# A four-layer f32 network on one core: the feed-forward part of layer 2 multiplied by quarters of the tokens, its anchors by another order of operands, and the last weights turned in layer 0

## The chip, the cores and the metric

The kernel runs on one core of a Trainium2 chip. A core has these engines: TensorE (PE; its weight loads are shown apart as PEld), VectorE (DVE), ScalarE (ACT), GpSimd (POOL) and SyncE (SP), of which SP and POOL issue the transfers of this kernel. The metric is device time in microseconds (us), the median of three runs. All arithmetic is in f32.

## The reference

The input x is 8 blocks of 128 tokens with 512 channels (8, 128, 512). Four layers follow, and each adds its result to x. A layer is a conditioning part and then a feed-forward part:

```
x = x + L0_ffn(L0_cond(x))   # gated FFN of width 1376 with a lora per block; then base_W + 8 lora experts, top 2
x = x + L1_ffn(L1_cond(x))   # an adapter chosen per block; then 8 heads weighed by a softmax
x = x + L2_ffn(L2_cond(x))   # attention, 32 heads, cached and new keys; then see below
x = x + L3_ffn(L3_cond(x))   # W + gated experts; then 64 experts of rank 8, top 16
```

The change is about layer 2's feed-forward part and about weights of layer 3. Layer 2's part takes y2, attention's result projected by Wo, and computes

```
H = y2 @ W.T + b                          # (1024 tokens, 512)
z = y2 @ A                                # rank 32
anchors = every second token              # the odd ones
H_slice = H[anchors, :8];  delta_slice = z[anchors] @ LiMEs.T
logits = 0.5 * H_slice / max|H_slice| + 0.5 * delta_slice / max|delta_slice|
probs = softmax(logits);  weights = probs * sigmoid((probs - second largest) / 0.5), normalized
p_mix = (weights repeated for both tokens of a pair) @ LiMEs
out = H + ((z * p_mix) @ Bmat) * 0.5
```

The two maxima are taken over all anchors, so no weight is known before every block's y2 is.

## The kernel before, in words

x lies in SBUF with channels on the partitions (4 chunks of 128) and the 1024 tokens along the free axis. A product with a 512x512 matrix is 4 output chunks by 4 input chunks of f32 matmuls for each group of tokens. One f32 matmul stands in the trace as two records.

**Layer 0** is `forward` from L48 on. Its big products are done by seven products of sums of sub-blocks in place of eight: the class `Down` (L601 to L636) has the steps `begin`, `go_on` and `out`, and the matmuls are issued at L367 (`dn`, `g`, `gu`, `td`). Its weights live in the pool `w0`, with tiles tagged "Ad" and "Bg" among others; SP loads them. L655 to L684 are the end of layer 0, where VectorE prepares sums for `Down` and then has idle stretches. After layer 0, attention's first operands q and l are loaded, VectorE forms sums of them (`q_s`), and PE's first use is `q_one` (L985).

**Attention** (L807, its loop `run` L1332) has 32 steps: 8 groups of heads by 4 pairs of token blocks. A step projects the next step's q, k and v (`project` L1019, by seven products in `seven` L971: `q_one` to `q_six`), turns them through DRAM (`turned_new` written, then read as `qT` and `kn` by `fetch` L1163; the cached keys through `turned_cached` as `kT`, L1120), computes scores `st` (`weigh` L1171), and mixes values into `av` (`mix` L1226). The softmax sums are formed by VectorE, written to DRAM (`sums`), and read back on all partitions as their reciprocals `R` (`inverted` L1212). `divided` (L1237) multiplies `av` by `R` into `oT`, `outputs` (L1243) adds sums of `oT` (`os`), and `leave` (L1251) projects these by Wo into y2, again by seven products (`wo_one` to `wo_six`, L985). The order of instructions on every queue is that of the program text wherever `kept` is put around an instruction. Attention has three PSUM tags: "mm" and "st" with 3 banks, "av" with 2.

**Work of layer 2 inside attention's last steps.** `ending` (L1747) holds all of layer 2's feed-forward part and layer 3. From step 5 on `run` advances `prepare` (L1790) at two places of a step: it turns the 512x32 matrix A by four PE transposes (`A2Tp`), copies it to `A2T`, multiplies with LiMEs (`alp`, 4 matmuls), and thus has WH = [W's first 8 columns, A·LiMEs], 16 columns that give both slices of an anchor at once. In the last group of heads each step turns two finished blocks of y2 (`turn` L1813, four PE transposes a block into `y2T`). The step before the last then does the first half of z and of the anchors:

```
if n + 2 == len(steps):
    end.low(0, bank)
    end.anchors(0, bank)
```

After the loop stand the last `divided`, `outputs`, `product(0, "st")` (block 0's H), and `leave(31)`.

**`low`** (L1821) computes z for four blocks at once: A's 32 columns are the weights, and each block goes to a slot of 32 partitions, N = 128 tokens. **`anchors`** (L1830) takes y2T as weights (128 tokens that are every second column) and streams WH's 16 columns; the result `hd` has tokens on partitions, as routing wants it. **`product(b)`** (L1847): 16 matmuls with N = 128 into one bank of `[P, 4, 128]`.

**`layer2`** (L2201) turns the last two blocks, does the second half of z and anchors, then products of blocks 1 to 3, with `weights_turned` (L1977) advanced between: layer 3's 512x512 `base3` and the 512x128 `wB3` are loaded during attention's end by `open3` (L1947) and turned by PE (`W3p`, 16 transposes in 4 banks, and `wB3p`, 4), each bank copied by ACT. Then `routing` (L1861: `big` maxima on VectorE, `top` over the partitions on POOL, softmax with ACT, top 2, sigmoid, `p`), `gains` (L1910: p turned by PE to `pT`, `pmix` = pT by LiMEs, `zp` = z·pmix/2), the product of block 4, `delta(0)` (L1934: Bmat's 32 rows by zp added into the banks of blocks 0 to 3, which VectorE then adds to x), blocks 5 to 7 with `fold_scores` (L1991: `qwp`, `qbp`, `fkp`, `gkp`, which need the turned weights), and `delta(1)`. Banks: block 0 to 2 take "st", 3 and 4 take "av", the rest "mm".

**`layer3`** (L2233) begins with the sums of W3 on POOL (`weights_summed`) and the router matmuls `midp` (`midp_l`, 32 records with 128x200 operands), then products by seven (`last_begun`, `last`), each with VectorE adding to x and SP storing to `out`. After `scores(1)`, `sums_checked` (L762) tests whether every softmax sum lay in a safe interval; its last instruction is VectorE's cast of the flag to an integer, `redo_i`. SP reads that flag, and only if it is set would attention be repeated by a slower path, which does not happen here.

## Time and profile before

| What | Value |
|---|---|
| Median of three runs | 1488.01 us (1486.08, 1488.01, 1489.38) |
| The profiled execution's own time | 1486.79 us |
| Its span, first to last instruction | 1485.0 us |
| Granted clock of PE, mean | 0.999 |
| VectorE busy | 1063.70 us (72%) |
| ScalarE busy | 563.59 us (38%) |
| GpSimd busy | 856.36 us (58%) |
| Bytes moved by DMA | 172.29 MB, mean 116 GB/s |

PE's busy time by stretches of the span:

| Stretch, us | What runs | PE busy, us | DVE busy, us |
|---|---|---|---|
| 0 to 300 | layers 0 and 1, attention's beginning | 297.96 | 152.06 |
| 300 to 1306 | attention's steps | 1004.05 | 810.55 |
| 1306 to 1336 | the end of the step before the last, the last step | 29.14 | 15.63 |
| 1336 to 1386 | the last projection and layer 2's feed-forward part | 49.09 | 20.31 |
| 1386 to 1485 | layer 3 | 91.08 | 65.16 |

How to read the rows that follow. In the list of groups a row has the line, the engine, the operation, the output and input by their names in the program, PE's tiles (128*32 is 128 rows by 32 columns of weights; 128x128 after it the streamed operand, partitions by elements), the count, and then the busy time and the mean duration of one in ns, and the engine's idle time ahead of them. In the timeline a row has its start and its length in us, engine, line, operation and count, and in brackets the idle time before it and what ended that. Matmuls overlap: a row's length is longer than the distance to the next row's start. "Start to start" below is that distance divided by the number of records.

### The profile page before, as it was taken

Reading aid. Unit: us, or ns where it says so; the run is one execution under the profiler, and the core shown is the slowest. Engines: PE = TensorE matmul, PEld = TensorE weight load, DVE = VectorE, ACT = ScalarE, POOL = GpSimd, SP = SyncE. Lnnn points to the kernel's source line nnn. Section 1 sums busy time; section 2 is a strip of 40 time slices with the busy share of each in tenths; the row PEclk is TensorE's granted clock in tenths of the full one; section 3 lists DMA queues with packets and bytes.
Section 4 is the critical chain, followed back from the end, with each engine's and each line's share of the span. In section 5 each row is a group of like instructions: output and inputs, shape, how many; then the busy total and the mean of one; then the engine's idle time right before and its main releaser. Section 6 shows DMA issues by size and latency. Waiting matters only on the chain.

```text
span 1485.0 us, 18055 instructions
## 1 busy us (share of the span) xinstructions
PE 1471.3 (99%) x5571; PEld 934.6 (63%) x5571; DVE 1063.7 (72%) x2121; ACT 563.6 (38%) x1426; POOL 856.4 (58%) x876
## 2 busy tenths in 40 slices
PE   9999999999999999999999999999999999999998
PEld 7888786455556555555655555555555555558886
DVE  4665425478878787787888778787878878855475
ACT  1111110044445544444554454554445455431110
POOL 2241105477767777776777777777777777622310
PEclk9999999999999999999999999999999999999999
DMA  7411001214555544453454455345445534433001
GB/s 242 121 44 32 23 1 62 88 41 126 183 158 148 153 131 128 150 181 117 135 157 129 128 167 172 107 135 164 129 124 165 170 107 137 120 107 98 1 8 52
DMA packets 155993, 172.29 MB, mean 116 GB/s; under 512 B 52784, under 2 KB 126256, under 8 KB 155760
## 3 DMA queue, kind: packets, MB, share of 16 engines
q1 hardware_dynamic: 137712, 134.04, 30.6%
q0 software_dynamic: 17056, 36.49, 7.8%
q8 instruction: 47, 0.77, 0.2%
q10 hardware_dynamic: 1120, 0.52, 0.1%
q14 instruction: 58, 0.48, 0.1%
HBM read 129.95 MB, written 40.76 MB: 115 GB/s over the span
## 4 chain that ended last, share of the span: by engine, by line
PE 94%; DVE 3%; DMA 1%; issue 1%; ACT 0%; SPq 0%; DVEq 0%; ACTq 0%
PE st L1179 18%; PE av L1231 17%; PE g L367 9%; PE q_six L985 8%; PE q_one L985 6%; PE q_five L985 6%; PE wo_two L985 5%; PE dn L367 5%; PE wo_one L985 4%; PE wo_six L985 3%; PE eo_l L53 3%; PE h L1767 2%; PE z L1767 2%; PE o L1767 1%; PE midp_l L53 1%; PE gu L367 1%
## 5 line engine op out<-in xcount | busy, mean ns | idle before, releaser
L928 POOL DMA_INDIRECT kn<-in_k_cache,kvrow_k x256 | 272.1, 1063 | 77.2 <-issue 70.3
L928 POOL DMA_INDIRECT vals<-in_v_cache,kvrow_v x256 | 271.4, 1060 | 73.6 <-issue 59.6
L1231 PE MATMUL av<-pT,vals 128*128 128x512 f32 x640 | 290.8, 592 | 0.2 <-DVE oT L1241 0.2
L1183 ACT ACTIVATE pT<-st,hide 128x512 f32<-128x512 f32 x256 | 175.9, 687 | 191.9 <-PE st L1179 164.3
L1179 PE MATMUL st<-qT,kT 128*128 128x512 f32 x512 | 236.2, 594 | 0.3
L1231 PEld LDWEIGHTS av<-pT,vals 128*128 128x128 f32 x640 | 121.4, 190 | 152.7 <-issue 149.5
L1084 POOL TENSOR_TENSOR vq<-q,txq 128x256 f32<-128x256 f32 x128 | 121.1, 976 | 132.9 <-ACT sqq L1058 93.4
L1179 PEld LDWEIGHTS st<-qT,kT 128*128 128x128 f32 x512 | 96.3, 190 | 110.2 <-issue 105.0
L1199 DVE TENSOR_TENSOR part<-pT 128x512 f32<-128x512 f32 x128 | 88.3, 691 | 77.6 <-ACT pT L1183 64.5
L985 PE MATMUL q_one<-q,x 128*128 128x384 f32 x256 | 93.0, 486 | 0.0
L1058 ACT ACTIVATE sqq<-q 128x128 f32<-128x128 f32 x252 | 78.2, 310 | 10.6 <-DVE q L1034 4.0
L985 PEld LDWEIGHTS q_one<-q,x 128*128 128x128 f32 x256 | 48.5, 190 | 39.8 <-issue 14.1
L985 PE MATMUL q_six<-q_s,xs_all 128*128 128x384 f32 x192 | 69.8, 486 | 0.0
L1039 ACT COPY q<-q_one 128x256 f32<-128x256 f32 x32 | 11.9, 372 | 151.8 <-PE q_one L985 133.5
L985 PE MATMUL wo_one<-o,oT 128*128 128x256 f32 x256 | 65.8, 379 | 0.7 <-DVE oT L1241 0.7
L1179 PE MATMUL st<-qT,kTn 128*128 128x512 f32 x128 | 65.4, 592 | 0.0
L985 PE MATMUL wo_two<-o_s,os 128*128 128x256 f32 x256 | 60.6, 380 | 0.3 <-DVE os L944 0.3
L1183 ACT ACTIVATE pT<-st,rs 128x512 f32<-128x512 f32 x64 | 44.0, 687 | 38.6 <-PE av L1231 13.4
L985 PEld LDWEIGHTS wo_one<-o,oT 128*128 128x128 f32 x256 | 48.6, 190 | 14.2 <-DVE oT L1241 0.8
L436 POOL TENSOR_TENSOR ws<-wu 128x256 f32<-128x256 f32 (+1 forms) x9 | 6.4, 712 | 86.5 <-DMA wu<-in_WuT 86.5
L1215 ACT COPY rows<-rows 32x32 f32<-32x32 f32 x96 | 20.7, 216 | 93.0 <-DVE rows L1210 89.7
L367 PE MATMUL g<-xs,ws 128*128 128x256 f32 (+1 forms) x240 | 55.1, 379 | 0.0
(466 smaller groups left out, 2832.5 us busy)
## 6 DMA issues: line engine op xcount, KB each, us to landing
turned_new<-qkt SPq DMA_DIRECT2D x120, 160.0 KB
turned_cached<-kt SPq DMA_DIRECT2D x128, 128.0 KB
kT<-turned_cached SPq DMA_DIRECT2D x32, 512.0 KB
R<-sums SPq DMA_DIRECT2D x32, 512.0 KB
qT<-turned_new SPq DMA_DIRECT2D x30, 512.0 KB
q<-in_WqT SPq DMA_DIRECT2D x8, 1024.0 KB
o<-in_WoT SPq DMA_DIRECT2D x8, 1024.0 KB
kn<-in_k_cache,kvrow_k POOLq DMA_INDIRECT x256
```

The source lines that it names most:

```text
L53: pe.matmul(o, lhsT, rhs, start=start, stop=stop)
L367: pe.matmul(o, lhsT, rhs, start=start, stop=stop, skip_group_check=True)
L928: kept(pool.indirect_dma_start(out=d[:, c, :], out_offset=None, in_=kc if what == "k" else vc, in_offset=bass.IndirectOffsetOnAxis(ap=kvro ...
L985: kept(pe.matmul(o, l[:, c, :], r[:, c, :], start=start and c == 0, stop=c == 1, skip_group_check=True))
L1058: kept(act.activation(sq, S[n][m][:, j, i, :], AF.Square, accum_out=S[n]["ssq"][:, j, col : col + 1]))
L1084: kept(pool.tensor_tensor(to, t[:, b, :, hi : hi + 64], wx[:, b, lo : lo + 64].unsqueeze(2).to_broadcast(list(to.shape)), ALU.mult,))
L1179: kept(pe.matmul(ps, s["kT"][:, c, 4 * j : 4 * j + 4, :] if c < 4 else s["kn"][:, j], s["qT"][:, :, REP * j : REP * (j + 1), :].rearrange( ...
L1183: kept(act.activation(pT[:, c, :, :].rearrange("p i t -> p (i t)"), ps, AF.Exp, **(dict(bias=hide[:, b, c : c + 1]) if c < 4 else dict(bia ...
L1199: kept(dve.tensor_tensor(o, l, r, ALU.add))
L1215: kept(act.copy(rows[0:32, g, :], rows[32 * g : 32 * g + 32, 0, :]))
L1231: kept(pe.matmul(ps, v[:, c, :], pT[:, c, :, :].rearrange("p i t -> p (i t)"), start=c == 0, stop=c == NC - 1, skip_group_check=True,))
L1767: return pe.matmul(o, lhsT, rhs, start=start, stop=stop, skip_group_check=True)
```

## The change

- **Product by quarters.** `product(q)` takes a quarter of the tokens (N = 256) and half of the output chunks to a bank `[P, 2, 256]`: two banks a quarter, 8 matmuls (16 records) each, 16 matmuls a quarter. Quarter 0 is done ahead of the last `leave`, where block 0 was; quarters 1 and 2 follow in `layer2`. Quarter 3's banks receive `delta` first and the product after it. The additions to x are apart (`added(q)`, two a quarter).
- **Anchors weights first.** WH is widened with zeros to 32 columns and becomes the weights; the tokens of a quarter (every second column of y2T, 128 of 256) are streamed, four quarters in the four slots of 32 partitions: `hdT`, 16 matmuls. VectorE copies it, PE turns it back in one transpose (`hd`), and VectorE adds the bias. `low` is done once for all tokens between the two (N = 256, four quarters in four slots), and ACT copies z. Nothing of z or the anchors is left in the step before the last.
- **`delta`, `pmix`** work on quarters too: N = 256 and 128, Bmat's 32 rows of each slot.
- **Last weights turned by VectorE in layer 0.** `base3`, `wB3` and A are loaded in layer 0 into the free tiles "Ad" and "Bg", turned in squares of 32x32 by VectorE's transpose (six instructions), and stored by SP to three tensors in DRAM in such an order that the whole is turned (24 stores, one for each 32 partitions). Three places of layer 0 advance this. `open3` loads W3 and wB3T from there, and `prepare` loads A2T from there, with `alp` a step later. The 24 PE transposes and ACT's six copies of them go.
- **The order in `layer2`**: anchors with z between, products of quarters 1 and (first half) 2 with routing beside them, pT, `qwp` and `qbp`, `pmix`, the rest of quarter 2, `delta`, three additions, quarter 3 with `fkp` and `gkp` between its halves.
- **The check's cast** to `redo_i` is issued behind the last gate operation of `scores(1)`.

The diff, without the lines that only pass arguments on; of longer removed stretches, which stand in the kernel above, only the first line is shown:

```diff
@@ -65,6 +65,20 @@
     x = xpool.tile([P, DC, NT], F32, tag="x", name="x")
+    w3T, wB3T, A2T = (
+        nc.dram_tensor(n, shape, F32, kind="Internal").ap()
+        for n, shape in (("w3_turned", (D, D)), ("wB3_turned", (D, P)), ("A2_turned", (32, D)))
+    )
+    late_weights = [
+        (a["base3"][d * P : (d + 1) * P, :], w3T[:, d * P : (d + 1) * P].rearrange("(b i) (q j) -> q i b j", i=32, j=32))
+        for d in range(DC)
+    ]
+    late_weights.append((a["wB3"], wB3T.rearrange("(b i) (q j) -> q i b j", i=32, j=32)))
+    late_weights.append((
+        a["A2"].rearrange("(c p) r -> p c r", p=P), A2T.rearrange("i (c q j) -> q i c j", q=4, j=32)
+    ))
+    late_turned = w3T, wB3T, A2T
@@ -577,6 +591,22 @@
+        def weights_turned():
+            for n in range(0, len(late_weights), 2):
+                ts = []
+                for i, (src, _) in enumerate(late_weights[n : n + 2]):
+                    t = w0.tile([P, 2, D], F32, tag=("Ad", "Bg")[i], name=f"late_{n + i}")
+                    m = math.prod(src.shape[1:])
+                    first = t[:, 0, :m]
+                    kept(sp.dma_start(first if len(src.shape) == 2 else first.rearrange("p (c j) -> p c j", j=src.shape[2]), src))
+                    ts.append((t, m))
+                for (_, dst), (t, m) in zip(late_weights[n : n + 2], ts):
+                    kept(dve.transpose(t[:, 1, :m], t[:, 0, :m]))
+                    for q in range(4):
+                        kept(sp.dma_start(dst[q], t[32 * q : 32 * q + 32, 1, :m].rearrange("i (b j) -> i b j", j=32)))
+                yield
         def ranks_to_ranks(wb1T):
@@ -658,8 +688,10 @@
         h_sums(0, ypool.tile([P, 3, NH, NT // 4], F32, tag="y", name="hs_0"), meanwhile)
-        for d in downs:
-            d.go_on()
+        turning = weights_turned()
+        downs[0].go_on()
+        next(turning)
+        downs[1].go_on()
         h_sums(1, st.tile([P, 3, NH, NT // 4], F32, tag="hs", name="hs_1", bufs=1), HB_.append)
@@ -668,11 +700,13 @@
         downs[0].go_on()
+        next(turning)
         mids0, route0, mix0, outs0 = experts("l0", wmr0, "probs", 2.0, None, wB0, base0, y0, add_to_x)[:4]
         mids0(0, psp_bank)
         route0(0)
         downs[1].begin()
         downs[1].go_on()
+        next(turning)
         for d in downs:
@@ -769,7 +803,8 @@
         pool.partition_all_reduce(anyone, some, P, bass_isa.ReduceOp.max)
-        dve.tensor_copy(redo_i, anyone)
+        with tc.issue_after(behind.ins):
+            dve.tensor_copy(redo_i, anyone)
@@ -1425,12 +1460,9 @@
                     end.turn(y2, 2 * (p - 1) + j, bank)
-            if n + 2 == len(steps):
-                end.low(0, bank)
-                end.anchors(0, bank)
         divided(n)
         every(outputs(n))
-        end.product(0, "st", bank)
+        end.product(0, ("st", "st"), bank)
         leave(n)
@@ -1779,22 +1811,21 @@
-    WH = early.tile([P, DC, 16], F32, tag="WH", name="WH")
+    WH = early.tile([P, DC, 32], F32, tag="WH", name="WH")
+    kept(pool.memset(WH[:, :, 16:32], 0.0))
     kept(sp.dma_start(WH[:, :, 0:8], chunks(a["W2T"])[:, :, 0:8]))
     b16 = early.tile([P, 16], F32, tag="b16", name="b16")
     kept(pool.memset(b16, 0.0))
     kept(sp.dma_start(b16[:, 0:8], a["b8"].partition_broadcast(P)))
-    zq = early.tile([P, TG, P], F32, tag="zq", name="zq")
+    zq = early.tile([P, NT // 4], F32, tag="zq", name="zq")
     hd = early.tile([P, NA, 16], F32, tag="hd", name="hd")
     def prepare(bank, room):
-        pt = bank("mm", [P, D], "A2Tp")
-        for c in range(DC):
-            kept(pe.transpose(pt[:32, c * P : (c + 1) * P], A2[:, c, :], ident))
         A2T = room([32, D], "A2T")
-        kept(act.copy(A2T, pt[:32]))
-        yield
+        kept(sp.dma_start(A2T, late_turned[2]))
+        for _ in range(3):
+            yield
         ps = bank("mm", [P, DC, 8], "alp")
@@ -1818,24 +1849,29 @@
-    def low(g, bank):
-        ps = bank("mm", [P, P], f"z2_{g}")
+    def quarter(q):
+        return slice(q * NT // 4, (q + 1) * NT // 4)
+    def low(bank):
+        ps = bank("mm", [P, NT // 4], "z2")
         for c in range(DC):
-            for j in range(HB):
...
+            for q in range(4):
+                mmq(ps[slot(q), :], A2[:, c, :], Y2T[0][:, c, quarter(q)], c == 0, c == DC - 1)
+        act.copy(zq, ps)
+    def anchors(bank, meanwhile):
+        ps = bank("mm", [P, P], "hdT")
+        for c in range(DC):
+            for q in range(4):
+                mmq(ps[slot(q), :], WH[:, c, :], Y2T[0][:, c, q * NT // 4 + 1 : (q + 1) * NT // 4 : 2], c == 0, c == DC - 1)
+        hdT = L3.w3.tile([P, P], F32, tag="hdT", name="hdTs")
+        dve.tensor_copy(hdT, ps)
+        meanwhile()
+        ps = bank("mm", [P, NA, 32], "hd")
+        pe.transpose(ps.rearrange("p q e -> p (q e)"), hdT, ident)
+        dve.tensor_tensor(hd, ps[:, :, 0:16], b16.unsqueeze(1).to_broadcast([P, NA, 16]), ALU.add)
@@ -1844,16 +1880,17 @@
-    def product(b, tag, bank):
...
+    def product(q, tags, bank, at=range(2), begun=False):
+        for i, tag in zip(at, tags):
+            ps = H[q, i] if begun else bank(tag, [P, 2, NT // 4], f"h_{q}_{i}")
+            for o in range(2):
+                for c in range(DC):
+                    mmq(
+                        ps[:, o, :], W["2"][:, c, (2 * i + o) * P : (2 * i + o + 1) * P], Y2T[0][:, c, quarter(q)],
+                        not begun and o == 0 and c == 0, begun and c == DC - 1,
+                    )
+            H[q, i] = ps
@@ -1915,34 +1952,36 @@
         act.copy(pT, pt[:8].rearrange("p i t -> p (i t)"))
-        pm = bank("mm", [P, TG, 64], "pmix")
...
+        yield
+        pm = bank("mm", [P, P], "pmix")
+        for q in range(4):
+            mmq(pm[slot(q), :], Li, pT[:, q * P : (q + 1) * P], True, True)
+        zp = L3.w3.tile([P, NT // 4], F32, tag="zp", name="zp")
         dve.scalar_tensor_tensor(
-            zp.rearrange("p g (t two) -> p g t two", two=2),
-            zq.rearrange("p g (t two) -> p g t two", two=2),
+            zp.rearrange("p (t two) -> p t two", two=2),
+            zq.rearrange("p (t two) -> p t two", two=2),
             0.5,
-            pm.unsqueeze(3).to_broadcast([P, TG, 64, 2]),
+            pm.unsqueeze(2).to_broadcast([P, P, 2]),
             ALU.mult,
             ALU.mult,
         )
         Z["zp"] = zp
-    def delta(g):
+    def delta(tags, bank):
         zp, Bm = Z["zp"], L3.Bm
-        for o in range(DC):
...
+        for i, tag in enumerate(tags):
+            H[3, i] = bank(tag, [P, 2, NT // 4], f"h_3_{i}")
+        for i in range(2):
+            for o in range(2):
+                for q in range(4):
+                    at = (2 * i + o) * P
+                    mmq(H[q, i][:, o, :], Bm[slot(q), at : at + P], zp[slot(q), :], q == 3 and o == 0, q < 3)
+    def added(q):
+        for i in range(2):
+            t = x[:, 2 * i : 2 * i + 2, quarter(q)]
+            dve.tensor_tensor(t, H[q, i], t, ALU.add)
@@ -1954,7 +1993,7 @@
             sp.dma_start(L3.Bm[slot(j), :], a["Bmat"])
-        L3.base = load("base3", [P, DC, D], chunks(a["base3"]))
+        L3.W = load("W3", [P, DC, D], chunks(late_turned[0]))
         L3.wq = w3.tile([P, DC, 32], F32, tag="Wq3", name="Wq3")
@@ -1962,7 +2001,7 @@
             sp.dma_start(L3.keys[32 * j : 32 * j + 16, :], a["keysT"])
-        L3.wB = load("wB3", [P, D], a["wB3"])
+        L3.wBT = load("wB3T", [P, DC, P], chunks(late_turned[1]))
         L3.wmr = w3.tile([P, DC, WR], F32, tag="wmr3", name="wmr3")
@@ -1973,20 +2012,6 @@
         return t
-    def weights_turned(bank):
...
@@ -2129,8 +2154,8 @@
         dve.reciprocal(s, s)
-        dve.tensor_tensor(gate, gate, s.unsqueeze(2).to_broadcast(n64), ALU.mult)
         gates[g] = gate
+        return dve.tensor_tensor(gate, gate, s.unsqueeze(2).to_broadcast(n64), ALU.mult)
@@ -2198,39 +2223,33 @@
-    def layer2(y2, bank, held=lambda: None, do=range(NB)):
+    def layer2(y2, bank, do=range(NB)):
         for b in do:
             turn(y2, b, bank)
-        for g in range(TG):
...
+        anchors(bank, lambda: low(bank))
         where = ["mm"]
-        def free(tag, shape, name):
...
+        folding = fold_scores(lambda tag, shape, name: bank(where[0], shape, name))
+        if (0, 0) not in H:
+            product(0, ("st", "st"), bank)
+        product(1, ("st", "av"), bank)
         routing()
-        gains(bank)
...
+        product(2, ("av",), bank)
+        gaining = gains(bank)
+        next(gaining)
+        next(folding)
+        next(gaining, None)
+        product(2, ("mm",), bank, range(1, 2))
+        delta(("mm", "mm"), bank)
+        for q in range(3):
+            added(q)
         where[0] = "st"
-        for b in range(HB + 1, NB):
...
+        product(3, ("mm",), bank, range(1), begun=True)
+        next(folding, None)
+        product(3, ("mm",), bank, range(1, 2), begun=True)
+        added(3)
+    def layer3(bank, between=lambda behind: None):
         mids, route, mix = L3.steps[:3]
@@ -2249,8 +2268,7 @@
         turned(0, bank)
-        scores(1, bank)
-        between()
+        between(scores(1, bank))
         last_sums(0, tile_of_w2)
```

## The prediction

> **What bounds the kernel now.** I read the page's first lines, then the chain that ended last, then TensorE's (PE's) groups with the shapes kept apart, and last the timeline of the stretches that the change touches.
>
> ```profile
> PE 1471.3 (99%) x5571; PEld 934.6 (63%) x5571; DVE 1063.7 (72%) x2121; ACT 563.6 (38%) x1426; POOL 856.4 (58%) x876
> ...
> PE 94%; DVE 3%; DMA 1%; issue 1%; ACT 0%; SPq 0%; DVEq 0%; ACTq 0%
> ```
>
> PE is busy 1471.3 of 1485.0 us and 94% of the chain that ended last is PE. So the time falls by what PE's instruction stream gets shorter, and rises by each wait that opens in it. Since busy matmuls overlap, I price PE by distance from start to start. An f32 matmul shows as two records, and I count records.
>
> ```profile
> L1767 PE MATMUL h<-y2T,WT 128*128 128x128 f32 x256 | 31.2, 277 | 0.0
> ...
> L53 PE MATMUL hd<-WH,y2T 128*128 128x16 f32 x32 | 4.6, 266 | 0.6 <-issue 0.5
> ...
> L367 PE MATMUL td<-h,AdT 128*32 128x256 f32 x80 | 4.5, 380 | 0.0
> ...
> L1767 PE MATMUL z<-y2T,A 128*32 128x128 f32 x64 | 3.9, 278 | 0.0
> ...
> L1983 PE MATMUL W3p<-ident,base 128*128 128x128 f32 x16 | 2.2, 273 | 0.0
> ```
>
> These are the operations that layer 2 changes, and one that stays (td). Each row's count by its busy time gives the price of a record: the anchors' matmuls (hd) cost 0.14 us although they stream only 16 columns, since each loads 128x128 weights. td streams 256 columns through 32 columns of weights in four slots side by side, at 0.05.
>
> The timeline gives the places.
>
> ```profile
> 1306.21 1.04 PE L1818 MATMUL y2T<-ident,y 128*128 128x128 f32 x8
> ...
> 1311.89 3.68 PE L1179 MATMUL st<-qT,kT 128*128 128x512 f32 x8
> ...
> 1335.64 1.04 PE L1818 MATMUL y2T<-ident,y 128*128 128x128 f32 x8
> ...
> 1340.90 1.13 PE L985 MATMUL wo_one<-o,oT 128*128 128x256 f32 x4 [0.65 <-DVE oT L1241]
> ...
> 1350.32 0.30 PEld L1767 LDWEIGHTS h<-y2T,WT 128*128 128x128 f32 x2 [0.20 <-issue]
> ...
> 1385.89 5.68 PE L53 MATMUL midp_l<-wmr,x 128*128 128x200 f32 x32
> ```
>
> Two stretches matter: 1306.21 to 1311.89, where the step before the last turns two blocks of y2 and does the first half of z and hd before its successor's scores (st); and 1335.64 to 1385.89, 50.25 us, the end of attention and all of layer 2. From 1385.89 on PE's order is the same in both kernels.
>
> **Prices of a record, start to start.** h with N 128: (1380.01-1376.33)/32 = 0.115. N 256 with full weights: (1346.04-1345.18)/4 = 0.216 (wo). Transposes: 0.11 (eight of W3p from 1360.28 to 1361.16). z, N 128 in four column slots: 26 records from 1352.44 to 1353.43, 0.038. Four column slots, N 256: td's 88 records from 166.44 to 171.33, 0.056. hd before: (1354.39-1353.43)/8 = 0.12. delta (h<-zp,Bm, 32 rows, N 128): 32 records from 1369.81 to 1370.91, 0.034. 32 rows, N 256: g<-tgm,Bg, 8 records from 158.35 to 158.86, 0.064.
>
> **The change part by part.**
>
> 1. *z and hd leave the step before the last.* Its eight transposes end their turn at 1306.21 + 8 x 0.108 = 1307.07; st then starts there and not at 1311.89: **-4.8 us**. What must be ready: qT's fetch was issued at 1300.41, and such fetches land 4.1 to 4.9 us later (the chain's rows at 526.01 and 1106.80), so by 1305.3. The reciprocal sums R were issued at 1307.72 and are used 6.56 us after st's start (1318.45 for 1311.89), so now at 1313.6, 5.9 us after the issue. In the step that begins at 1111.81 R was issued at 1112.45 and used 5.9 us later without a wait. So it just holds; if not, up to 4.8 us come back.
>
> 2. *The stretch to layer 3.* Before, by these prices: 16 y2T 1.7, 28 wo 6.05, 256 h 29.4, 20 W3p and wB3p 2.2, 32 z 1.2, 16 hd 1.9, 64 delta 2.2, pT 0.43, 16 pmix 0.36, qwp 0.88, qbp 0.33, fkp and gkp 1.06: 47.7. The other 2.55 of the 50.25 are waits: 0.95 around 1340.9 and 1342.5 for R, oT and os, 1.6 at the copies of y2T and at changes between narrow and full weights. After: y2T 1.7, wo 6.05, 128 h x 0.216 = 27.65, 32 hdT x 0.038 = 1.2, 32 z x 0.056 = 1.8, the transpose back 0.1, 32 delta x 0.064 = 2.05, pT 0.43, 8 pmix 0.25, qwp 0.88, qbp 0.33, fkp and gkp 1.06: 43.5. The 0.95 goes: quarter 0's products are now 32 x 0.216 = 6.9 us long where block 0's were 3.7, so PE reaches wo_one 3.2 us later behind R, and DVE's os is done. Left at copies and switches: 1.6 as before. So 45.1, **-5.1 us**. Of this h gives 1.75, the turned weights 2.2, z and hd together 0.1 (their larger part was in point 1).
>
>  Not shown before: matmuls that stream every second column (hdT). Between 0.034 (delta) and 0.056 (as if all 256 were read), 1.1 to 1.8 us; I take z's 0.038, the same count of columns. delta's 32 rows with N 256 lie between twice 0.034, with four rows side by side, and the 0.089 of all 72 records of g<-tgm,Bg (6.4 us); 2.05 to 2.85. h's N 256 can hardly differ from wo's.
>
>  [...]
>
> 3. *Does routing keep up?* It runs on DVE, ACT and POOL beside h. hd's addition comes at 1354.58 before. In the new order I count 20.7 us from the stretch's start to it (y2T, h, wo, the first h of quarter 1, hdT, z, transpose); then 0.5, 3.75 (big at 1355.29 to m at 1359.04), 0.3 for ACT, which no longer has W's copies ahead of m (these held it to 1361.93), and 2.2 (1362.21 to 1364.41): 27.4. PE reaches pT after 29. Cover 1.5 us; beyond that each us is lost, since PE's queue behind pT holds qwp, pmix, delta and all later h. ACT's copy of pT (0.57) lies behind qwp and qbp (1.2). The order puts POOL's top ahead of W3's sums.
>
> 4. *Weights turned in layer 0.* Six DVE transposes, five of 128x512 at 0.70 (partT at 1297.59) and a small one, 3.7 us in all, stand in DVE's idle times of 12.2 us (to 190.70), 11.9 (to 221.95) and 6.3 (to 237.90). SP gets 6 loads and 24 stores; its queue is empty from 163.8 to 238.47. The last eight stores follow a transpose at about 231.5, take 8 x 0.44 to issue, as turned_cached's do (4 in 1.76), and land some 2.0 us on (297.15 to kT's issue at 300.93): 237 to 239, where attention's first loads are issued (238.47). If late, those loads and POOL's tables slip; the weights' first reader, DVE at 246.21, works for PE's 291.07. Nothing, -0 to +0.5.
>
> 5. *The rest.* A2's four transposes leave the attention step: **-0.43 us** (alp, same length, a step later; A2T's load costs SP 0.4 us ahead of turned_cached, which is fetched two steps early). The check's cast left DVE idle 2.82 us to 1376.31, while its next work waited for PE until 1385.98: nothing either way; 0.15 us of DVE now stands at about 1443 (old clock) with 0.4 us before PE needs the next sum. SP's read of the flag moves ahead of the first output store, which is 35 us from the end.
>
> Sum: -4.8 - 5.1 - 0.4 = -10.3 us, with the switches a little more: **-10.5**. The profiled execution took 1486.8 us (span 1485.0): 1476.3. The three runs' median is 1488.0, 1.2 above it; I say **1476.5**.
>
> **Rivals.**
>
> - *The wait moves, part of the gain is lost.* R misses 1313.6, or routing misses its 1.5 us, or delta and hdT cost their upper bounds (0.8 and 0.6). For it: R's 5.9 us have one precedent only. Against: R alone stands ahead in SP's queue of the 2 MB that follow. Loss 2 to 5 us: 1478.5 to 1481.5.
> [...]
> - *Narrow matmuls with N 256 don't run side by side* (96 records of hdT, z and delta at 0.115 and 0.216 are 17.5 us for 5.05): +12.4, 1488.7, no change. td's row speaks against.
> - *Slower: the attention steps begin to wait for qT.* Its place is st's start in 28 steps; fetched at 1073.92 for 1079.27, 5.35 us with a landing of 4.1 to 4.9, slack about 0.9 (at 1111.81 it was 0.3 late already). Three new tensors in DRAM shift turned_new, and a fetch slower by 0.9 + x us costs 28x; from x = 0.4 on all gain is gone, at 0.8 the time is 1498.7. Nothing in the trace makes these transfers longer: their size and rows stay.
>
> **How the numbers follow.** Forecast 0.66 (1474.8 to 1478.5), part lost 0.20, more gained 0.08, no side by side 0.02, qT 0.04. Measurement tells 0.2% (3 us) from no change. Faster 0.94, same 0.02, slower 0.04. For 8 in 10 the range leaves the far ends out: 1472.5 to 1481.5.
>
> **What would show it.** st of the last step starts 4.6 to 5 us sooner after its y2T, with no wait at av for R; 128 records of h at N 256, 0.216 apart; no wait at wo_one; 44 to 46 us from the second y2T to midp; pT without wait; DVE's six transposes in layer 0 with PE's starts up to 290 unchanged. I am wrong if PE shows idle time ahead of av, pT or qwp, or if steps grow from 32.24 us.

## The result, and the profile after

| | Before | After |
|---|---|---|
| Median of six runs each | 1486.38 us (1485.66 to 1489.38) | 1476.10 us (1473.63 to 1478.06) |
| Ratio of the times | 1 | 0.9927, 95% interval 0.9913 to 0.9941 |
| The profiled execution, its span | 1486.79, 1485.0 us | 1478.06, 1476.2 us |

The kernel is 10.3 us faster by the medians, and by the interval of the ratio 8.8 to 12.9 us. The forecast was 1476.5 us. The first lines of the page of the changed kernel (busy time by engine, and the chain that ended last):

```profile
PE 1462.2 (99%) x5348; PEld 922.4 (62%) x5348; DVE 1063.5 (72%) x2125; ACT 561.2 (38%) x1421; POOL 851.1 (58%) x877
PE 95%; DVE 2%; DMA 1%; issue 1%; ACT 0%; SPq 0%; POOL 0%; DVEq 0%
```

PE is as full as it was (99% busy) and has 223 records less, 5348 for 5571; it bounds the kernel as before. The timeline of PE, changed kernel, at the two places that the prediction named:

```profile
1307.02 1.04 PE L1849 MATMUL y2T<-ident,y 128*128 128x128 f32 x8
1307.90 3.60 PE L1214 MATMUL st<-qT,kT 128*128 128x512 f32 x8
...
1331.57 1.04 PE L1849 MATMUL y2T<-ident,y 128*128 128x128 f32 x8
1332.44 7.07 PE L1799 MATMUL h<-y2T,WT 128*128 128x256 f32 x32
1339.35 1.03 PE L1020 MATMUL wo_one<-o,oT 128*128 128x256 f32 x4
...
1360.21 0.60 PE L1952 MATMUL pT<-ident,p 128*8 128x128 f32 x4
...
1376.23 4.05 PE L53 MATMUL midp_l<-wmr,x 128*128 128x200 f32 x23
```

The last step's scores (st) start 0.88 us behind the first row's start, where it was 5.68 us before: 4.80 us gone. The stretch from the second y2T to midp is 1376.23 - 1331.57 = 44.66 us, where it was 50.25: 5.59 us gone. No row of the stretch has a bracket, so the profile shows no wait of PE in it, not at wo_one and not at pT. The two places together gave 10.39 us. The one wait between them is that of av for oT at 1315.12, 0.19 us, as long as in the kernel before.

The spans of these two profiles differ by only 8.8 us. The other 1.6 us lie outside these places, in the main at two: PE's first q_one came at 291.84 instead of 291.07 (a gather of layer 0, Au, landed late and PE waited 0.88 us at 18 us), and the span ended 7.04 us behind PE's last matmul, where it was 6.05. The first experiment asks whether these belong to the change.

From here on "the stretch" is this one, from the second y2T to midp; it comes out to 0.01 us where the same work is done (44.66, 44.67 and 44.66 in after, again and cast_free), while times move by four us and more from run to run. So the length of the stretch decides between theory and rival, and the time confirms it where it can.

| Kernel | Stretch, us | Median, us | Ratio to the kernel before, with interval |
|---|---|---|---|
| before | 50.25 | 1486.38 | 1 |
| after | 44.66 | 1476.10 | 0.9927 (0.9913 to 0.9941) |
| again | 44.67 | 1475.66 | 0.9936 (0.9923 to 0.9950) |
| blocks128 | 45.76 | 1477.05 | 0.9948 (0.9934 to 0.9961) |
| pe_turns_no_layer0 | 46.85 | 1478.77 | 0.9959 (0.9945 to 0.9972) |
| pe_turns_with_layer0 | 46.86 | 1477.22 | 0.9945 (0.9932 to 0.9959) |
| first_half_later | 52.25 | 1484.74 | 0.9980 (0.9967 to 0.9994) |
| tokens_as_weights | 47.46 | 1481.33 | 0.9958 (0.9945 to 0.9971) |
| cast_free | 44.66 | 1477.05 | 0.9927 (0.9914 to 0.9940) |
| z_with_h_between | 45.73 | 1476.74 | 0.9928 (0.9915 to 0.9942) |
| quarter0_half_ahead | 45.82 | 1476.76 | 0.9936 (0.9923 to 0.9950) |
| routing_late | 51.77 | 1482.41 | 0.9967 (0.9954 to 0.9980) |
| routing_late_less | 49.20 | 1480.63 | 0.9952 (0.9938 to 0.9965) |
| routing_late_least | 46.42 | 1478.34 | 0.9950 (0.9937 to 0.9964) |

Kernels were measured on different chips, each beside the kernel before, so medians of different rows are compared by their ratios.

### The profile page after: what moved, and what is told of

It reads as the page before. It is cut to its first block, busy times and chain, and to the rows that moved or that the text cites. A ratio compares the mean times of both kernels' runs of the same rounds, so it can differ in the third digit from the quotient of the medians.

```text
span 1476.2 us, 17664 instructions
## 1 busy us (share of the span) xinstructions
PE 1462.2 (99%) x5348; PEld 922.4 (62%) x5348; DVE 1063.5 (72%) x2125; ACT 561.2 (38%) x1421; POOL 851.1 (58%) x877
## 4 chain that ended last, share of the span: by engine, by line
PE 95%; DVE 2%; DMA 1%; issue 1%; ACT 0%; SPq 0%; POOL 0%; DVEq 0%
PE st L1214 18%; PE av L1266 18%; PE g L381 9%; PE q_six L1020 8%; PE q_one L1020 6%; PE q_five L1020 6%; PE wo_two L1020 6%; PE dn L381 5%; PE wo_one L1020 4%; PE wo_six L1020 4%; PE eo_l L53 3%; PE h L1799 2%; PE z L1799 2%; PE midp_l L53 1%; PE o L1799 1%
## 5 line engine op out<-in xcount | busy, mean ns | idle before, releaser
L963 POOL DMA_INDIRECT vals<-in_v_cache,kvrow_v x256 | 267.9, 1046 | 73.6 <-issue 60.5
L1093 ACT ACTIVATE sqq<-q 128x128 f32<-128x128 f32 x252 | 78.2, 310 | 10.4 <-DVE q L1069 3.7
L1250 ACT COPY rows<-rows 32x32 f32<-32x32 f32 x96 | 20.7, 216 | 92.8 <-DVE rows L1245 79.1
```

Of the source, the lines that this page charges most:

```text
L963: kept(pool.indirect_dma_start(out=d[:, c, :], out_offset=None, in_=kc if what == "k" else vc, in_offset=bass.IndirectOffsetOnAxis(ap=kvro ...
L1093: kept(act.activation(sq, S[n][m][:, j, i, :], AF.Square, accum_out=S[n]["ssq"][:, j, col : col + 1]))
L1250: kept(act.copy(rows[0:32, g, :], rows[32 * g : 32 * g + 32, 0, :]))
```

## The experiments

The theory: the time is PE's stream, and each part of the change is worth its records at their start-to-start prices. The rivals, named in the expectations, are that the gain came from waits and changes of tile rather than from work, that the turning in layer 0 costs time, and chance. A change of tile, or "change" for short, is the passage from matmuls with full 128*128 weights to narrow ones (32 columns or 32 rows) or back.

### The changed kernel once more: again

No edit.

> The changed kernel once more. The time fell by 10.3 us between the medians, but the two profiled spans differ by only 8.8: the two stretches of PE that the change touches gave 4.80 and 5.59 us, and 0.8 us came back before attention (a gather of layer 0 landed late at 18 us and PE's first q_one stood at 291.84 instead of 291.07) and 1.0 us behind the last matmul (7.0 us from its end to the span's end instead of 6.05). Theory chance: neither belongs to the change; this profile shows PE free of a wait at 18 us, first q_one within 0.3 us of 291.07 and some 6 us behind the last matmul, and the time is 0.990 to 0.995 of the kernel before. Rival, the turning in layer 0 and the new tensors in DRAM cost these 1.8 us: both come again in this profile, and the difference of spans stays near 8.8.

The stretch was 44.67 us, and the span 1474.6, 10.4 below that of before. First q_one stood at 291.51 (PE waited 0.68 us early in layer 0, now for x), 7.00 us lay behind the last matmul. So chance did not show itself as the expectation had it: the wait moved to another load, and the long tail came again. Over all kernels' profiles it did: the early wait ran from 0 to 2.44 us, for Au, for x, or for nothing that the profile names, and the kernels without any turning in layer 0 have it too (0.34 us in pe_turns_no_layer0, 0.46 in first_half_later). With the kernel before, where there was no such wait, these are only three profiles, though, and seven of the eleven others have 0.62 us and more, so it is not shown that the new tensors have no part in it. As to the end, the tail behind PE's last matmul ran from 5.3 (pe_turns_no_layer0) to 7.5 us (blocks128), and routing_late, whose stores are those of the changed kernel, has 5.45. And from attention's first scores to the first y2T of the timeline above, 991.90 us before and 991.93 after, the profiles range from 989.6 (quarter0_half_ahead) to 996.6 us (first_half_later, which does nothing else there than the kernel before). A spread of this size, in a part where these kernels differ by A's four transposes alone, hides what is smaller.

### Products in blocks of 128: blocks128

```diff
-                for c in range(DC):
-                    mmq(ps[:, o, :], W["2"][...], Y2T[0][:, c, quarter(q)], ...)
+                for b in range(2):
+                    for c in range(DC):
+                        mmq(ps[:, o, b * P : (b + 1) * P], W["2"][...],
+                            Y2T[0][:, c, (2 * q + b) * P : (2 * q + b + 1) * P], ...)
```

> The changed kernel with its products in N = 128 again: each matmul of 256 tokens becomes two of 128, in the same banks and the same order. Theory, PE's stream is the time: 256 records at 0.115 for 128 at 0.216, 1.8 us more; the stretch from the second y2T to midp grows from 44.66 to 46.4 us and the time to about 1477.9 where the changed kernel has 1476.1. Rival, the width does not matter since the weight loads lie beside the matmuls: stretch and time as in the changed kernel, and the 1.8 us came from elsewhere.

The stretch was 45.76 us, 1.10 more, not 1.8. PE's timeline of this kernel, quarter 0:

```profile
1332.18 7.31 PE L1799 MATMUL h<-y2T,WT 128*128 128x128 f32 x64
1339.32 1.03 PE L1020 MATMUL wo_one<-o,oT 128*128 128x256 f32 x4
```

64 records in 1339.32 - 1332.18 = 7.14 us are 0.1116 each, where the forecast had 0.115; 32 of N 256 take 6.91. So the width matters, and it is worth 256 x 0.1116 - 128 x 0.216 = 0.9 us and a little at the ends. The forecast had the direction of this term right and its size too large.

### The weights turned by PE again: pe_turns_no_layer0 and pe_turns_with_layer0

```diff
+        turning = weights_turned(...)      # W3p and wB3p as before, on PE, copies by ACT
+        next(turning)
-        product(1, ("st", "av"), bank)
+        product(1, ("st",), bank, range(1))
+        next(turning)
+        product(1, ("av",), bank, range(1, 2))
+        next(turning)
         routing()
         product(2, ("av",), bank)
+        for _ in turning:
+            pass
```

The first kernel also has nothing of the turning in layer 0 and turns A by PE in attention, as before; the second keeps layer 0's turning and A's copy from DRAM.

> The changed kernel with the last weights turned by PE in layer 2 again (20 transposes and five copies by ACT) and A turned by PE in attention (4 transposes), and with nothing turned in layer 0: its loads, VectorE's transposes and stores are gone. Theory, PE's stream: 20 x 0.11 = 2.2 us more in the stretch (46.9 us), 0.4 more in attention, and layer 0 as it was: 2.6 us more than the changed kernel, about 1478.7, unless routing is held up by the copies on ACT (it was 2.5 us early at pT, and gets 2.2 us of transposes more). Rival, the turning in layer 0 cost 0.8 us or more: the first q_one comes 0.8 us sooner than in the changed kernel, and the time is at most 1.8 us above it.

> As the kernel above (PE turns the last weights in layer 2), but layer 0 still turns and stores all three, and only A's copy is read from there. Theory, PE's stream: 2.2 us more than the changed kernel, about 1478.3, and 0.4 less than the kernel above, all of it from A's four transposes; layer 0's starts on PE are equal in both. Rival, layer 0's turning costs PE time: this kernel is slower than the one above.

Both stretches are 2.2 us longer, 46.85 and 46.86, as 20 transposes at 0.11 make it. PE's timeline of pe_turns_no_layer0 at the last of them:

```profile
1362.23 0.60 PE L2025 MATMUL wB3p<-ident,wB 128*128 128x128 f32 x4
1362.67 0.60 PE L1950 MATMUL pT<-ident,p 128*8 128x128 f32 x4
```

pT follows without a bracket: routing, held 1.3 us by the copies on ACT in pe_turns_with_layer0 (p at 1358.7), is still early. As to layer 0, the two medians (0.9959 and 0.9945) differ by less than their intervals and with the wrong sign for the rival: the kernel without the turning is not faster. In the traces, from PE's td to its first q_one it is 291.07 - 166.44 = 124.63 us before and 291.84 - 167.66 = 124.18 after, and 290.57 - 166.39 = 124.18 in pe_turns_no_layer0, which turns nothing there. So the turning in layer 0 costs PE nothing in that part. A's four transposes (0.4 us) are below what these runs can tell.

### One part alone in the kernel before: first_half_later

```diff
-            if n + 2 == len(steps):
-                end.low(0, bank)
-                end.anchors(0, bank)
...
-            if g or len(do) > HB:
-                low(g, bank)
-                anchors(g, bank)
+            low(g, bank)
+            anchors(g, bank)
```

> The kernel before with one part alone: the first half of z and of the anchors leaves the step before the last and stands with the second half in layer 2, same form, same matmuls. The forecast booked 4.8 us for this place, but by the prices 32 records of z (0.038) and 16 of hd (0.12) are only 3.1 us of work; 1.7 us were waits for the copies of y2T and switches. Theory: the scores of the last step start 4.8 us sooner after y2T, the stretch of layer 2 grows by 3.1, and the time falls by 1.7 us. Rival one, the waits come with the work (there are copies of y2T ahead of it there too): no change. Rival two, the stretch had room for the work beside its waits: 4.8 us faster.

The scores start 0.88 us behind y2T (1310.84 and 1309.96), 4.80 sooner, and the stretch grew by 2.00 us to 52.25: 2.80 net, and the time was 0.9980 of that before, some 3.0 us less (0.9 to 4.9 by the interval). All three numbers of the expectation missed; the theory's was nearest. Why 2.0 and not 3.1 shows in PE's timeline:

```profile
1348.89 1.08 PE L1764 MATMUL z<-y2T,A 128*32 128x128 f32 x32
1349.91 2.06 PE L53 MATMUL hd<-WH,y2T 128*128 128x16 f32 x16
1351.89 1.08 PE L1764 MATMUL z<-y2T,A 128*32 128x128 f32 x32
1352.90 2.06 PE L53 MATMUL hd<-WH,y2T 128*128 128x16 f32 x16
1354.81 4.93 PE L1764 MATMUL h<-y2T,WT 128*128 128x128 f32 x42
```

Both halves take 1354.81 - 1348.89 = 5.92 us in four blocks of one kind each. In the kernel before they took 4.80 in the step and 3.96 in the stretch (1349.98 to 1354.39, less four records of h among them), 8.76 together, cut into pieces by waits for the copies of y2T and by other work put between, with changes at each cut. So 2.8 us of what the change gained at the anchors and z was not work at all: it comes from doing the same matmuls in one piece, where nothing is late. How it divides between waits and changes is not shown.

### The old form of the anchors at the new place: tokens_as_weights

```diff
+        ps = bank("mm", [P, NA, 16], "hd")
+        for i in range(NA):
+            for c in range(DC):
+                mm(ps[:, i, :], Y2T[0][:, c, 256 * i + 1 : 256 * i + 256 : 2], WH[:, c, 0:16], ...)
+        meanwhile()
-        ... hdT, its copy, its transpose
```

> The changed kernel with the anchors in the old form at the new place: y2T as weights, 16 columns of WH streamed, 16 matmuls (32 records), no copy and no transpose back. Theory, each record is bound by its 128x128 weight load: 32 x 0.12 = 3.8 us for the 1.35 us of hdT and its transpose, 2.5 us more; stretch 47.1 us, time about 1478.6. Rival, the loads lie beside z's matmuls in the new order: under 1 us more.

The stretch was 47.46 us, 2.80 more. z and the anchors took 6.28 us (1351.01 to 1357.29), against 3.49 in the changed kernel (1347.66 to 1351.58, less 0.43 of h). PE's timeline of the changed kernel, and then the longest of the rows of this one:

```profile
1347.66 0.43 PE L1799 MATMUL hdT<-y2T,WH 128*32 128x128 f32 x6
1348.01 0.70 PE L1799 MATMUL h<-y2T,WT 128*128 128x256 f32 x2
1348.64 0.99 PE L1799 MATMUL hdT<-y2T,WH 128*32 128x128 f32 x25
...
1349.58 1.90 PE L1799 MATMUL z<-y2T,A 128*32 128x256 f32 x29
1351.41 0.33 PE L1873 MATMUL hd<-ident,hdTs 128*128 128x128 f32 x1
1351.58 8.80 PE L1799 MATMUL h<-y2T,WT 128*128 128x256 f32 x40
```

```profile
1351.01 2.90 PE L53 MATMUL hd<-WH,y2T 128*128 128x16 f32 x24
```

24 records in 2.82 us (the next row starts at 1353.83) are 0.118 each, for 16 columns streamed. The form of the matmuls is worth 2.8 us here, and their place was worth 2.8 in the experiment above. Together z and the anchors gave 5.3 us (8.76 to 3.49), so about half is form and half is place; the two halves come from different kernels and need not add up to a tenth.

### More changes between narrow and full weights: z_with_h_between

```diff
         for c in range(DC):
             for q in range(4):
                 mmq(ps[slot(q), :], A2[:, c, :], Y2T[0][:, c, quarter(q)], ...)
+            between()      # one h matmul of quarter 1, taken from product(1)
```

> The changed kernel with one full-width h matmul behind each of z's four groups of four narrow ones: six more changes between narrow and full weights, the same matmuls. What stood at such changes in the changed kernel's stretch is its length less its records at their prices. Theory, a change costs about 0.1 us (the first full-width matmul behind hd and behind pmix came 0.1 to 0.2 us late): the stretch grows from 44.66 to 45.2 or 45.3. Rival, only waits for copies cost and changes are free: 44.7. [...] Routing is 1.7 us later by the h matmuls put ahead of it, inside its 2.46 us of cover. Time 0.5 us above the changed kernel, not to be told from it by the runs; the trace decides.

The stretch was 45.73 us, 1.07 more for six changes, 0.18 each: above the theory's 0.1. PE's timeline of this kernel:

```profile
1351.05 0.70 PE L1799 MATMUL h<-y2T,WT 128*128 128x256 f32 x2
1351.68 0.64 PE L1799 MATMUL z<-y2T,A 128*32 128x256 f32 x8
1352.25 0.70 PE L1799 MATMUL h<-y2T,WT 128*128 128x256 f32 x2
```

The two records of h last 0.63 us from start to start where they take 0.43 among their like, and z's eight 0.57 where their price makes 0.45. No row has a bracket, so nothing is waited for. So a change costs by itself. Record by record, h's first start comes 0.31 us behind the last of z, its second 0.32 behind the first, and z follows 0.31 behind that, where h's records among their like are 0.216 apart: the larger part of the cost falls on the way from narrow to full weights. Only this one kind of change, between h and z, was priced.

### Half of quarter 0 ahead of the projection: quarter0_half_ahead

```diff
-        end.product(0, ("st", "st"), bank)
+        end.product(0, ("st",), bank, range(1))
...
+        product(0, ("st",), bank, range(1, 2))
```

> The changed kernel with only the first half of quarter 0's product ahead of the last projection, 16 records or 3.45 us, as long as block 0's were before; the other half stands behind. Theory, the 0.95 us of waits at wo_one and wo_two come back (R lands 4 us after its issue whatever stands there): the stretch grows to 45.6. Rival, the scheduler's order fills the gap with an h matmul that was to be done anyway, so that only 0.2 to 0.5 comes back.

```profile
1333.51 1.13 PE L1020 MATMUL wo_one<-o,oT 128*128 128x256 f32 x4 [0.60 <-DVE oT L1276]
```

The wait at wo_one is back in PE's timeline, 0.60 us, and the stretch is 45.82 us, 1.16 more: the theory's 0.95 and a little. The rival fell: an h matmul was put in between, and the gap opened all the same. What removed these waits in the change is that quarter 0's product is 3.3 us longer than block 0's was (6.91 for 3.57).

The brackets understate what such a wait costs. The same part of PE's timeline in the kernel before, and the row that ends it in the changed kernel:

```profile
1336.51 3.74 PE L1767 MATMUL h<-y2T,WT 128*128 128x128 f32 x32
...
1341.87 0.38 PE L1767 MATMUL h<-y2T,WT 128*128 128x128 f32 x2
1342.51 1.97 PE L985 MATMUL wo_two<-o_s,os 128*128 128x256 f32 x8 [0.26 <-DVE os L944]
...
1347.77 0.38 PE L1818 MATMUL y2T<-ident,y 128*128 128x128 f32 x2
```

```profile
1345.39 0.38 PE L1849 MATMUL y2T<-ident,y 128*128 128x128 f32 x2
```

From the first h to this y2T it is 11.26 us before, for 34 records of h and 28 of wo that take 34 x 0.1116 + 6.04 = 9.83 among their like: the two waits cost 1.43 us, where the brackets (0.65 and 0.26) add up to 0.91. In the changed kernel it is 12.95 us (from 1332.44) for 6.91 + 6.04, so nothing is lost; in quarter0_half_ahead 11.08 (1329.29 to 1340.37) for 9.93, so 1.15 are.

### The cast not held: cast_free

```diff
-        with tc.issue_after(behind.ins):
-            dve.tensor_copy(redo_i, anyone)
+        dve.tensor_copy(redo_i, anyone)
```

> The changed kernel with the cast of the check's flag no longer held behind the gates: it stands on VectorE ahead of the last two additions of layer 2, and its operand comes from POOL at 1377.6 us, six us after VectorE would reach it. Theory: the additions slip from 1371.9 to 1377.8, but what reads them starts on PE at 1399 and on POOL at 1393, so no change in time. Rival, the additions free PSUM banks or x that PE needs: PE waits between midp and fp, up to 2 us, and the hold was worth that.

VectorE's timeline of this kernel:

```profile
1376.51 0.15 DVE L806 CAST redo_i<-anyone 128x1 int32<-128x1 f32 x1 [6.06 <-POOL anyone L805]
```

VectorE stood idle for 6.06 us ahead of the cast, and the last two additions of layer 2 came behind it. The stretch (44.66) and the part from midp to PE's end (92.95 us, in the changed kernel 92.93) are what they were: no change, as the theory and the prediction had it. Holding the cast gained nothing.

### How much cover routing has: routing_late, routing_late_less, routing_late_least

The cover is the time by which routing's result p is ready before PE reaches pT.

```diff
+        for _ in range(24):      # 20, 16
+            dve.tensor_scalar(hd, hd, 1.0, None, ALU.mult)
         big = new("big", [P, 2])
```

> The changed kernel with 24 small multiplications by one ahead of routing's first maximum on VectorE, one behind the other (24 x about 0.22 = 5.3 us; they change no value). Theory: routing was ready 2.5 us before PE's pT (p at 1357.7, pT at 1360.2), so PE waits 2.8 us at pT and the time grows by 2.8; forecast's cover was 1.5, by which it would grow by 3.8. Rival, the order has other work for PE: less than 1 us.

The stretch was 51.77 us, 7.1 more and not 2.8 or 3.8. PE's timeline of routing_late:

```profile
1363.05 1.01 PE L1954 MATMUL pT<-ident,p 128*8 128x128 f32 x4 [4.12 <-DVE p L1946]
1363.99 1.94 PE L1799 MATMUL qwp<-W,Wq 128*32 128x512 f32 x8
```

The wait is 4.12 us: the multiplications took 5.74, the scheduler moved four operations of the check ahead of routing's next step (0.83 us), and 2.46 of cover went first. The other 3.0 us lie behind the wait: pT takes 1.01 us for 0.60, qwp 1.94 for 1.07. The table of stretches shows why. A row has the stretch, its length, the busy time of PE, PEld, DVE, ACT and POOL in us, and then the granted clock, the share of full speed at which the profile says PE ran:

```profile
1363.00:1365.00 2.00, 1.95 (x12) 0.72 (x16) 0.00 (x0) 0.57 (x1) 0.94 (x2) 0.50 0.03 8
1365.00:1367.00 2.00, 2.00 (x25) 0.58 (x17) 0.00 (x0) 0.75 (x2) 2.00 (x4) 0.50 0.00 0
...
1369.00:1372.00 3.00, 3.00 (x23) 2.42 (x25) 0.00 (x0) 0.00 (x0) 0.57 (x1) 1.00 0.00 0
```

The granted clock is 0.50 behind the wait, and 1.00 again from 1369 on. Two more kernels ask how long a wait must be for that.

> As routing_late with 20 multiplications instead of 24. There PE waited 4.12 us at pT (5.74 us of multiplications and 0.83 of the check's operations that moved ahead, less 2.46 of cover), and the records of the next 4.5 us took twice their time, with a granted clock of 0.50: 3.0 us more. Theory, it is the length of the wait that halves the clock, and a shorter one does not: 4.8 us of multiplications, at most 0.8 of the check, less 2.46: PE waits 2.3 to 3.1 us, the records behind keep 0.11 and 0.216, and the stretch is 47.0 to 47.8. Rival, any wait halves the clock afterwards: 50 us.

This theory fell. PE waited 2.61 us, and the clock was halved here too (a row of PE's timeline, then one of the table of stretches):

```profile
1361.76 0.60 PE L1954 MATMUL pT<-ident,p 128*8 128x128 f32 x4 [2.61 <-DVE p L1946]
```

```profile
1364.00:1366.00 2.00, 2.00 (x16) 1.29 (x12) 0.42 (x1) 0.60 (x2) 2.00 (x4) 0.50 0.00 0
```

The stretch was 49.20 us: 44.66, the wait of 2.61, and 1.93 of half clock. By rows of a quarter us of the same table, the granted clock of routing_late_less falls at 1362.78 and comes back at 1366.19, 3.41 us later; in routing_late it falls at 1361.95 and comes back at 1368.77, 6.82 us later.

> As routing_late with 16 multiplications. With 24 and 20 of them PE waited 4.12 and 2.61 us, and the granted clock then stood at 0.50 for 6.8 and for 3.4 us, which cost 3.0 and 1.9 us more than the wait; a stretch of 3.4 us that was idle for 2.4 of them went before the fall with 20. Here 3.65 to 3.85 us of multiplications (0.23 to 0.24 each) and 0.3 to 0.5 of the check's operations that stand among routing's now, less 2.46 of cover, give a wait of 1.5 to 1.9 us. [...] Rival, any wait above 1 us is enough: the clock falls here too and the stretch is 47.7 to 48.5.

```profile
1360.55 0.60 PE L1954 MATMUL pT<-ident,p 128*8 128x128 f32 x4 [1.58 <-DVE p L1946]
```

PE waited 1.58 us, within the 1.5 to 1.9 expected, the granted clock is 1.00 in every row of the table of stretches from 1340 to 1367, and the stretch is 46.42 us, 44.66 plus 1.58 and 0.18. The rival fell.

## Why the prediction was right, point by point

| Term | Forecast, us | Measured, us | By |
|---|---|---|---|
| 1. Step before the last | -4.8 | -4.80 | both timelines |
| 2. h with N 256 | -1.75 | -1.10 | blocks128 |
| 2. Turned weights | -2.2 | -2.19 | pe_turns, both |
| 2. Waits at wo_one and wo_two | -0.95 | -1.43 | start to start, 11.26 for 9.83; quarter0_half_ahead gives back 1.16 |
| 2. Rest of the stretch | -0.2 | about -0.9 | what is left of -5.59 |
| 3. Cover of routing | 1.5 | 2.46 | p ready at 1357.75, pT at 1360.21 |
| 4. Layer 0 | 0 to +0.5 | 0 | td to q_one, 124.63 and 124.18 |
| 5. A's transposes | -0.43 | not to be told | pe_turns |
| 5. Cast | 0 | 0 | cast_free |

The mechanism was right: PE's stream is the time, and what the change takes out of it comes off the time. The sum of the two places, -10.39 us, is 0.5 us more than the forecast's -9.9. That it is so near is partly luck, since three terms of the stretch were mis-sized, one to one side and two to the other. A's 0.43 us, the last term of the sum, is below what these runs can tell.

**h was taken 0.65 us too high.** Its price of 0.115 came from a row that begins behind qbp's narrow weights: 3.68 us for 32 records hold 32 x 0.1116 = 3.57 and 0.11 for a change. A price from a row with a change at its edge books the change to every record. It also hid the waits and changes of the kernel before: 256 records at 0.1116 are 0.9 us less than the 29.4 booked for them, so the waits and changes were 3.4 us there, not 2.55.

**The waits at wo_one and wo_two were taken 0.5 us too low**, since 0.95 is about what the brackets show, and the starts are 1.43 us late.

**"Left at copies and switches: 1.6 as before" was wrong** by some 0.7 us. It keeps the cost of the changes, where the rows of PE's timeline give 16 of them before and 9 after, with the passage from qbp's 32 columns to pmix's 8 rows counted as one. At the 0.18 us of z_with_h_between, seven changes fewer would be 1.3 us, more than the 0.9 that is left. A count that comes to 16 takes in both sides of pT, whose four records take 0.44 us before (1364.72 to 1365.16), 0.11 each like other transposes, so nothing was lost there; without these two it is five changes fewer, an estimate of 0.9. The forecast's sum has 0.2 us for it, "with the switches a little more": no run shows that term, and what the runs showed in its place is 0.18 us for each change between h and z. h's smaller gain kept the time near the forecast.

**Why step 1 gave 4.8** was not asked closely enough. Of the 4.8 us booked there, 3.1 by the prices were matmuls that the new order must do in layer 2, and the rest went in waits and changes. The booking came out since the new form (3.49 us for all of z and the anchors) is not much longer than the 3.1 that the prices gave: hdT 32 records at 0.037 (forecast 0.038, so streaming every second column of 256 costs here what 128 columns were priced at), z 0.061 with its changes (forecast 0.056), and delta 1.94 us (2.05). In that form z and the anchors of all blocks take less than their second half took in the kernel before (3.96).

**R held**, as forecast: its load was issued at 1307.42, and VectorE read it from 1314.38 on, 7.0 us later, without a wait. By how much it held is not shown.

**Rivals.** That part of the gain would be lost again fell: no wait appeared, and routing had 1 us more cover than worked out, since hd came 20.2 us into the stretch, not 20.7, and p 5.97 us behind it, not 6.7. That narrow matmuls with N 256 would not run side by side fell: z and delta stand at 0.061 us a record, and h, with as many columns and full weights, at 0.216. That attention would wait for qT fell: PE waited 0.2 us for qT in all steps of this profile, and the steps' total is that of before (991.93 and 991.90 us).

## What to carry to other kernels

Where one engine is busy throughout, price an edit by start-to-start distances within rows that have no change of tile at an edge, and count the changes as a term of their own: between h and z they cost 0.18 us each, about as much as one to two records of h. Price a wait by the same distances, since its bracket leaves a part out (0.91 for 1.43 us). Work that stands between two producers' copies costs its waits as well as its records; about half of what z and the anchors gave came from doing the same matmuls later in one piece. When a wait is added on TensorE, or the cover of one gets thin, look also at the granted clock of the records behind it: here 1.58 us of wait cost 1.76, 2.61 cost 4.54, and 4.12 cost 7.11, the last two with 0.50 behind them.

## What the runs showed of the hardware that was not expected

The granted clock fell to one half at a wait of 2.61 us, for 3.41 us (routing_late_less, 1.00 from 1340 to 1362), and at one of 4.12 us for 6.82, twice that (routing_late, 1.00 from 1350 to 1361). With 4.12 us it fell 1.10 us ahead of pT's start (1361.95 and 1363.05), with 2.61 us 1.02 us behind it (1362.78 and 1361.76). It did not fall at 1.58 us (routing_late_least). Three early waits in layer 0 go the same way by the times of the records: behind 2.17 us for x in z_with_h_between the first four records of gu take 1.62 us from start to start and the next four 1.71, where their like take 0.86 (from 10.10 to 10.96), and behind 2.44 us for Au in pe_turns_with_layer0 the four of AuT take 0.90, where they take 0.44 without a wait (17.01 to 17.44 in the kernel before); behind 1.46 us for Au in tokens_as_weights the same four take 0.50 and the next four of gu 0.87. So of these six waits the four of 2.17 us and more have slow records behind them, and those of 1.46 and 1.58 have none. What lies between, and what sets the 3.41 and 6.82 us, is not shown.

GpSimd stood idle for some 6 to 7 us between its reductions over partitions and its plain additions, with nothing that the profile names to wait for: in the changed kernel 7.13 us from the end of top (1352.83) to W3s (1359.96), in routing_late_least 7.22 there, in cast_free 5.68 from the last W3s to anyone, in the kernel before 5.76 ahead of anyone and 6.87 behind it. Nothing on PE's path waited for it here. The cause is not shown, and the profile's spans on GpSimd are rough.
